# Two graph layers on one core: exps and scalings moved into later rounds, the change of layers and the end laid out anew

## The chip, the cores and the metric

The kernel runs on one core of a Trainium2 chip. The metric is the device time of one execution in microseconds; before the change the median of three runs is 2457.41 us (2450.8 to 2460.89). Engines are named as in the profile: PE multiplies matrices (PEld loads its weights), DVE is the vector engine, ACT the scalar engine, POOL is GpSimd, and SP only issues DMAs (SPq). Each engine works through its own instructions in order; across engines they wait on semaphores.

## The reference

There are 128 graphs of 128 nodes with 512 features. Layer 0 is attention with a two-step propagation, layer 1 scores every node against its graph and scales a projected value by a softmax over the nodes. All numbers are float32.

```python
# layer 0
h = relu(layernorm(x))
Xw = h @ Wv + bv;  sj = Xw @ aw[:d, 0];  si = Xw @ aw[d:, 0]
e = leaky_relu(sj[:, None, :] + si[:, :, None] + ab[0], 0.2)
alpha = A * exp(e);  transition = alpha / (sum(alpha, -1) + 1e-12)
H = 0;  Xk = h
for k in range(3):
    H = H + Xk @ Wk[k] + bk[k]
    Xk = einsum('bij,bjd->bid', transition, Xk)
x = x + relu(H)
# layer 1
h = relu(layernorm(x))
q, k = split(h @ Wqk);  v = h @ Wv1
agg = einsum('bij,bjd->bid', adj, k * mask)
w = mask / sqrt(512) * einsum('bid,bid->bi', q, agg)
x = x + softmax(w, axis=1)[:, :, None] * v
```

## The kernel before

Layer 0 goes through 64 pairs of graphs and writes to DRAM, for each pair: h of layer 1 (H2D), its transposed blocks (XD), the transposed adjacency (ATD) and x after layer 0 (X1D).

Layer 1 goes through 32 quads (two pairs, four graphs), `q` from 0 to 31. Its products h @ [M, Wv1], where M joins both score weights, are done with Strassen's scheme at two levels. The outer level has seven factors (1, 5, 2, 6, 3, 7, 4), the inner one seven products (p1, p5, p6, p2, p7, p3, p4). A quad has two rounds: the first takes factors 1 and 5 in the PSUM banks a1, b1, c1, e1 and, step by step beside it, 2 and 6 in a2, b2, c2, e2; the second takes 3 and 7, and 4. Each step is one product of both sets.

```python
def one_round(q, banks, factors, s, ends):
    ...
    def p1():
        product(a, 1, True)
        nc.scalar.copy(b, a)
    def p5():
        product(e, 5, True)
        nc.scalar.copy(s[:, 0], e)
    def p6():
        product(b, 6)
        nc.scalar.copy(c, b)
    def p2():
        product(a, 2)
        ends[0, 0](v[0])
    def p7():
        product(c, 7)
        nc.scalar.copy(s[:, 1], c)
        ends[1, 1](v[3], sv[:, 1])
    def p3():
        product(b, 3)
        ends[0, 1](v[1], sv[:, 0])
    def p4():
        product(c, 4)
        ends[1, 0](v[2])
```

The ends of set 2 are additions: DVE adds the PSUM bank into s, POOL adds that to c (`two`), or DVE adds the bank to c at once (`one`). So ACT copies between banks, and PE needs these copies for its next steps.

The left operands: `load_left(q)` loads four blocks of f by the SP queue and lets POOL form four sums; `inner_sums` lets DVE form the inner level's operands `in` from f. f has two buffers, one for even and one for odd quads.

```python
def weights(w, pw):                      # softmax factors of a quad
    nc.vector.tensor_reduce(peak, pw, AX.X, OP.max, negate=True)
    for j in range(g2):                  # four graphs
        nc.scalar.activation(ej, pw[:, j, :], AF.Exp, bias=peak[:, j:j + 1], accum_out=w[:, 2, j:j + 1])
    nc.vector.tensor_add(w[:, 3], w[:, 0], peak)
    nc.scalar.activation(w[:, 4], w[:, 3], AF.Exp)
    nc.vector.reciprocal(w[:, 5], w[:, 2])
    nc.vector.tensor_mul(w[:, 3], w[:, 4], w[:, 5])

def spread_scores(col):                  # scores to DRAM and back, to every partition: pwd, pw
    ...
def scaled(q):
    factors = weights(W.pop(q), PW.pop(q))
    for pair in range(2):
        for j in range(G):
            nc.scalar.activation(v, v, AF.Copy, scale=factors[:, at:at + 1])

def store(q):
    for pair in range(2):
        nc.gpsimd.dma_start(v, X1D[p].rearrange("g n d -> n g d"), accum_op=OP.add)   # c += x1
        nc.sync.dma_start(out[p * G:(p + 1) * G].rearrange("b n d -> n b d"), v)

for q in range(NQ):
    together(one_round(q, set1, (1, 5), ...), one_round(q, set2, (2, 6), ...))
    done["v"] = nc.gpsimd.tensor_add(outer[0], outer[3], outer[1]).ins               # "v"
    if q > 1:
        behind("v", store, q - 2)
    for i, bank in enumerate((a1, a2, e1, e2)):                                     # agg
        ordered(nc.tensor.matmul, bank, AT[q][:, pair, j], H2[q][:, pair, j], ...)
        nc.scalar.copy(agg[:, pair, j], bank)
    if q + 1 < NQ:
        load_rest(q + 1)                                                            # h2, at
        inner_sums(q + 1, early, 0, 4)
    scores(q, 0, c[:, 2])
    together(one_round(q, set1, (3, 7), ...), one_round(q, set2, (4,), ...))
    nc.gpsimd.tensor_add(outer[1], outer[3], outer[1])
    if q + 2 < NQ:
        load_left(q + 2, fpools[q % 2])
    if q + 1 < NQ:
        inner_sums(q + 1, back, 4, 3)
    scores(q, 1, c[:, 2])
    PW[q] = spread_scores(W[q])
    if q > 0:
        behind("score", scaled, q - 1)
scaled(NQ - 1)
for q in (NQ - 2, NQ - 1):
    store(q)
```

c, in which a quad's result is built, has three buffers. The order on each engine is not the order of the program text: a scheduler places the instructions by priority and by what they need, and `behind` and `ordered` hold it to an order.

Of the kernel before, what the change touches and what calls it, by code (L numbers as in the profile page):

```python
# [15 lines left out]
def kernel(  # L16
# [25 lines left out]
    nc = tc.nc  # L42
# [34 lines left out]
                                      ("a1", "b1", "c1", "e1", "a2", "b2", "c2", "e2"))  # L77
    set1, set2 = (a1, b1, c1, e1), (a2, b2, c2, e2)

    def behind(what, op, *args):  # L80

        with tc.issue_after(done[what]):
            return op(*args)

    def ordered(op, *args, **how):

# [375 lines left out]
    def y10(p, steps):  # L462

        s = front.tile([P, 2, WP * 2], FP, name="s", bufs=1)[:, :, :D]

        def end12(b, t):
            done["c12"] = behind("left" if p else "t", nc.vector.tensor_add, b, b, t).ins

        strassen(set1, LEFT.pop(p), right10, s, False, {
            (0, 0): lambda a: None,  # L470
            (1, 1): lambda e, t: behind("left" if p else "t", nc.vector.tensor_add, e, e, t),
            (0, 1): end12,
            (1, 0): lambda c: None}, steps)

# [76 lines left out]
    for p in range(NP):  # L551
        def lefts():
            if p == 0:
                behind("t", begin, 1)
                behind("left", norm0, 2)
                return
            if p + 2 < NP:
                behind("t", begin, p + 2)
            if p + 3 < NP:
                behind("left", norm0, p + 3)  # L560

        if p > 1:
            behind("x1", attention, p)
        y10(p, {1: lefts, 6: lambda: t_transposed(p)})
        if p > 0:
            behind("c12", for_layer1, p - 1)
        z = inner(p)
        if p == 0:
            y2(1)
            spread_columns(1)  # L570
            attention(1)
        outer(p, z)
        if p == 0:
            begin(2)
            norm0(3)
            setup_ctx.close()
            stage_ctx = ExitStack()
            stage = stage_ctx.enter_context(tc.tile_pool(name="stage", bufs=2, side="right"))
        if p + 2 < NP:
            y2(p + 2)  # L580
        if p + 1 < NP:
            seed_a()
            seed_e()
        norm2(p)
        if p + 4 < NP:
            load_x(p + 4)
        if p + 3 < NP:
            load_adj(p + 3)
        if p == 2:
            rightl = combine({(kh, k): rl[:, kh * HC:(kh + 1) * HC, k] for kh in range(2)  # L590
                              for k in range(2)}, [tl[:, i] for i in range(4)])
        if 3 <= p < 3 + len(FACTORS):
            prepare(FACTORS[p - 3], stage)
        if p == 3 + len(FACTORS):
            stage_ctx.close()
            prep_ctx.close()
            early = ctx.enter_context(tc.tile_pool(name="early", bufs=1, side="right"))
            RW = {}
            for o in FACTORS[:4]:
                RW[o] = early.tile([P, 7, HD], FP, name=f"rw{o}")  # L600
                nc.sync.dma_start(RW[o], RWD[o])
# [42 lines left out]
    load_left(0, early)  # L644
    inner_sums(0, early, 0, 4)
    layer0.close()
    back = ctx.enter_context(tc.tile_pool(name="back", bufs=1))
    fpools[1] = back
    for o in FACTORS[4:]:
        RW[o] = back.tile([P, 7, HD], FP, name=f"rw{o}")  # L650
        nc.sync.dma_start(RW[o], RWD[o])

    def load_rest(q):
        H2[q] = back.tile([P, 2, G, D], FP, name="h2", bufs=2)
        AT[q] = back.tile([P, 2, G, N], FP, name="at", bufs=2)
        for i in range(2):
            p = 2 * q + i
            nc.sync.dma_start(H2[q][:, i], H2D[p].rearrange("g n d -> n g d"))
            nc.sync.dma_start(AT[q][:, i], ATD[p])

    def one_round(q, banks, factors, s, ends):

# [11 lines left out]

        def p1():
            product(a, 1, True)
            nc.scalar.copy(b, a)

        def p5():
            product(e, 5, True)  # L680
            nc.scalar.copy(s[:, 0], e)

        def p6():
            product(b, 6)
            nc.scalar.copy(c, b)  # L685

        def p2():
            product(a, 2)
# [1 line left out]

        def p7():
            product(c, 7)
            nc.scalar.copy(s[:, 1], c)  # L693
            ends[1, 1](v[3], sv[:, 1])

        def p3():
# [8 lines left out]

    def plain_ends(to):

        return {(0, 0): lambda a: nc.scalar.copy(to(0, 0), a),
                (1, 1): lambda e, t: nc.vector.tensor_add(to(1, 1), e, t),
                (0, 1): lambda b, t: nc.vector.tensor_add(to(0, 1), b, t),  # L710
                (1, 0): lambda c: nc.scalar.copy(to(1, 0), c)}

    def adding_ends(to, other):

        def one(i, j):
            return lambda a: nc.vector.tensor_add(to(i, j), a, other(i, j))  # L716

        def two(i, j):
            def end(e, t):
                nc.vector.tensor_add(t, e, t)  # L720
                nc.gpsimd.tensor_add(to(i, j), t, other(i, j))  # L721
            return end

        return {(0, 0): one(0, 0), (1, 1): two(1, 1), (0, 1): two(0, 1), (1, 0): one(1, 0)}

    def together(*rounds):
        for steps in zip(*rounds):
            for step in steps:
                step()

    def weights(w, pw):

        g2 = 2 * G
        w = w[:, :6 * g2].rearrange("p (k g) -> p k g", g=g2)
        peak = small.tile([P, g2], FP, name="peak")
        nc.vector.tensor_reduce(peak, pw, AX.X, OP.max, negate=True)
        for j in range(g2):
            ej = back.tile([P, N], FP, name="ej", bufs=2)
            nc.scalar.activation(ej, pw[:, j, :], AF.Exp, bias=peak[:, j:j + 1],  # L739
                                 accum_out=w[:, 2, j:j + 1])  # L740
        nc.vector.tensor_add(w[:, 3], w[:, 0], peak)
        nc.scalar.activation(w[:, 4], w[:, 3], AF.Exp)
        nc.vector.reciprocal(w[:, 5], w[:, 2])
        nc.vector.tensor_mul(w[:, 3], w[:, 4], w[:, 5])
        return w[:, 3]

    def spread_scores(col):

# [6 lines left out]
        nc.sync.dma_start(dst.rearrange("p g n -> p (g n)"), bcast(d, 0, 2 * G * N))  # L755
        return dst

    C, W, PW = {}, {}, {}

    def scores(q, pair, y):  # L760

        for j in range(G):
            junk = back.tile([P, D], FP, name="junk", bufs=1)
            b, at = (2 * q + pair) * G + j, pair * G + j
            done["score"] = nc.vector.scalar_tensor_tensor(
                junk, agg[:, pair, j], wscale[:, b:b + 1], y[:, j].rearrange("p h d -> p (h d)"),
                op0=OP.mult, op1=OP.mult, accum_out=W[q][:, at:at + 1]).ins

    def scaled(q):

        factors = weights(W.pop(q), PW.pop(q))
        for pair in range(2):
            for j in range(G):
                v = C[q][:, pair, j].rearrange("p h d -> p (h d)")
                at = pair * G + j
                nc.scalar.activation(v, v, AF.Copy, scale=factors[:, at:at + 1])  # L776

    def store(q):

# [4 lines left out]
            nc.gpsimd.dma_start(v, X1D[p].rearrange("g n d -> n g d"), accum_op=OP.add)  # L784
            nc.sync.dma_start(out[p * G:(p + 1) * G].rearrange("b n d -> n b d"), v)

    load_rest(0)
    inner_sums(0, back, 4, 3)
    load_left(1, back)
    for q in range(NQ):  # L790

        c = C[q] = back.tile([P, 4, G, 2, HD], FP, name="c", bufs=3)
        W[q] = wcols[q % 3]
        s1 = back.tile([P, 2, D], FP, name="s1", bufs=1)
        s2 = back.tile([P, 2, D], FP, name="s2", bufs=1)
        agg = back.tile([P, 2, G, D], FP, name="agg", bufs=1)
        outer = [c[:, i].rearrange("p j h d -> p (j h d)") for i in range(4)]

        together(one_round(q, set1, (1, 5), s1, plain_ends(lambda i, j: c[:, 0:2, i, j])),
                 one_round(q, set2, (2, 6), s2, adding_ends(  # L800
                     lambda i, j: c[:, 2:4, i, j],
                     lambda i, j: c[:, 0:1, i, j].to_broadcast([P, 2, HD]))))

        done["v"] = nc.gpsimd.tensor_add(outer[0], outer[3], outer[1]).ins
        if q > 1:
            behind("v", store, q - 2)
        for i, bank in enumerate((a1, a2, e1, e2)):
            pair, j = divmod(i, 2)
            ordered(nc.tensor.matmul, bank, AT[q][:, pair, j], H2[q][:, pair, j], start=True, stop=True)
            done["agg"] = nc.scalar.copy(agg[:, pair, j], bank).ins  # L810
        if q + 1 < NQ:
            load_rest(q + 1)
            inner_sums(q + 1, early, 0, 4)
        scores(q, 0, c[:, 2])

        together(one_round(q, set1, (3, 7), s1, adding_ends(lambda i, j: c[:, 0::3, i, j],
                                                            lambda i, j: c[:, 0::3, i, j])),
                 one_round(q, set2, (4,), s2, adding_ends(lambda i, j: c[:, 2:3, i, j],
                                                          lambda i, j: c[:, 3:4, i, j])))

        nc.gpsimd.tensor_add(outer[1], outer[3], outer[1])
        if q + 2 < NQ:
            load_left(q + 2, fpools[q % 2])
        if q + 1 < NQ:
            inner_sums(q + 1, back, 4, 3)
        scores(q, 1, c[:, 2])
        PW[q] = spread_scores(W[q])
        if q > 0:
            behind("score", scaled, q - 1)
    scaled(NQ - 1)  # L830
    for q in (NQ - 2, NQ - 1):
        store(q)


# [23 lines left out]
```

## Time and profile before

One execution of the kernel before spans 2452.7 us, with a mean granted PE clock of 0.971. Busy time by engine (its share of the span counts all stages together):

| engine | busy us | share | instructions |
|---|---|---|---|
| PE | 2284.0 | 93% | 8223 |
| DVE | 1694.6 | 69% | 4191 |
| ACT | 1246.3 | 51% | 2929 |
| POOL | 865.2 | 35% | 854 |

Layer 0 lasts until about 1471 us, layer 1 from there to the end. By stretches of 300 us within layer 1 (1520 to 2420), PE is busy for 266 to 269 us, DVE for 236 to 242, ACT for 157 and POOL for 195 to 205; the granted clock is 0.95 to 0.97 there and 1.00 in layer 0 from 100 to 1440 us. In a table of windows a share is read within its own stage; a wait in brackets in the timeline gives the idle time before an instruction and what ended it.

### The profile page before, as it was taken

What the parts mean: (1) busy time and instruction counts of PE and PEld (TensorE: products, weight loads), DVE (VectorE), ACT (ScalarE), POOL (GpSimd) and SP (SyncE); (2) the same over time, 40 slices, a digit from 0 to 9 for tenths busy, and PEclk for the clock granted to TensorE, in tenths of its full rate; (3) what the DMA queues carried; (4) which work ended last, traced back from release to release, by engine and by line L of the source; (5) the groups of instructions that cost most, each with busy time, mean ns of one, the idle gap of its engine ahead of it and who ended that gap; (6) DMA issues with size and microseconds to landing.
All of it is one profiled execution on the core that took longest, in us unless ns stands there. A gap on an engine that the chain in (4) does not pass through costs nothing.

```text
span 2452.7 us, 29079 instructions
## 1 busy us (share of the span) xinstructions
PE 2284.0 (93%) x8223; PEld 1563.6 (64%) x8223; DVE 1694.6 (69%) x4191; ACT 1246.3 (51%) x2929; POOL 865.2 (35%) x854
## 2 busy tenths in 40 slices
PE   8899999999999999999999997888888889998884
PEld 4566656566666666666666665677776777777773
DVE  5676666666666666666666655878887777788784
ACT  3455545455555555555555543555555555555553
POOL 3011111211111111111111104666666666667663
PEclk8999999999999999999999998999999999899997
DMA  7566786667666666666666645466666555555665
GB/s 201 176 201 197 219 262 202 179 189 202 196 184 184 193 204 189 180 192 198 200 185 183 188 136 192 126 171 166 168 168 171 157 158 155 155 155 163 167 159 124
DMA packets 379011, 440.95 MB, mean 180 GB/s; under 512 B 35342, under 2 KB 233614, under 8 KB 378850
## 3 DMA queue, kind: packets, MB, share of 16 engines
q1 hardware_dynamic: 347344, 386.23, 51.5%
q0 software_dynamic: 31504, 52.87, 11.8%
q8 instruction: 65, 1.06, 0.2%
q14 instruction: 96, 0.79, 0.1%
q10 hardware_dynamic: 2, 0.00, 0.0%
HBM read 256.33 MB, written 182.65 MB: 179 GB/s over the span
## 4 chain that ended last, share of the span: by engine, by line
PE 73%; DVE 10%; ACT 6%; DMA 5%; issue 3%; POOL 2%; SPq 1%; ACTq 0%; POOLq 0%; DVEq 0%
PE a L88 22%; PE c L88 20%; PE b L88 19%; PE e L88 12%; DVE in L633 2%; ACT ej L739 2%; DVE s L720 2%; DMA c<-x1d 2%; DMA f<-xd 1%; POOL c L721 1%; DVE in L631 1%; ACT c L776 1%; DVE c L716 1%; DVE in L632 1%; ACT s L693 1%
## 5 line engine op out<-in xcount | busy, mean ns | idle before, releaser
L108 POOL DMA_DIRECT2D agb<-in_adj_dram x256 | 148.4, 586 | 754.9 <-DVE aT L436 712.5
L88 PE MATMUL a<-r,x 128*128 128x512 f32 (+1 forms) x1024 | 376.4, 490 | 8.7 <-DVE x L320 8.6
L721 POOL TENSOR_TENSOR c<-s,c 128x512 f32<-128x512 f32 x192 | 225.5, 1189 | 235.5 <-DVE s L720 181.2
L88 PEld LDWEIGHTS a<-r,x 128*128 128x128 f32 x1024 | 191.0, 192 | 88.9 <-issue 62.3
L88 PE MATMUL b<-rw,in 128*128 128x256 f32 x896 | 239.1, 412 | 0.0
L88 PE MATMUL a<-rw,f 128*128 128x256 f32 x896 | 214.3, 379 | 0.0
L88 PEld LDWEIGHTS b<-rw,in 128*128 128x128 f32 x896 | 187.7, 210 | 30.6
L88 PE MATMUL c<-rw,in 128*128 128x256 f32 x448 | 122.9, 406 | 85.7 <-ACT c L685 85.7
L88 PEld LDWEIGHTS a<-rw,f 128*128 128x128 f32 x896 | 170.2, 190 | 36.8 <-issue 14.6
L88 PE MATMUL b<-t,sx 128*128 128x257 f32 (+1 forms) x512 | 187.7, 489 | 4.6 <-ACT b L360 4.6
L88 PE MATMUL c<-t,x 128*128 128x257 f32 (+1 forms) x512 | 187.0, 487 | 2.5 <-ACT s L368 2.5
L88 PE MATMUL c<-t,sx 128*128 128x257 f32 (+1 forms) x512 | 188.5, 491 | 0.2 <-ACT c L364 0.2
L88 PE MATMUL e<-t,sx 128*128 128x257 f32 (+1 forms) x512 | 187.0, 488 | 0.0
L88 PE MATMUL b<-r,sx 128*128 128x257 f32 (+1 forms) x512 | 186.4, 486 | 0.0
L320 DVE STREAM_TRANSPOSE x<-hv 128x512 f32<-128x512 f32 x254 | 165.3, 688 | 23.5 <-DMA hv<-hd 13.6
L276 DVE BATCH_NORM_STATS2 st<-xg 128x6 f32<-128x512 f32 x128 | 82.3, 684 | 135.1 <-DMA xg<-in_x_dram 135.1
L88 PEld LDWEIGHTS c<-rw,in 128*128 128x128 f32 x448 | 85.8, 197 | 108.7 <-ACT c L685 97.8
L368 ACT COPY s<-c 128x257 f32<-128x257 f32 (+1 forms) x128 | 60.6, 473 | 174.5 <-PE c L88 174.2
L88 PEld LDWEIGHTS b<-t,sx 128*128 128x128 f32 x512 | 97.6, 192 | 74.4 <-issue 60.5
L88 PEld LDWEIGHTS c<-t,sx 128*128 128x128 f32 x512 | 97.5, 191 | 71.8 <-issue 61.6
L88 PEld LDWEIGHTS c<-t,x 128*128 128x128 f32 x512 | 94.6, 189 | 74.8 <-issue 60.5
L88 PEld LDWEIGHTS e<-t,sx 128*128 128x128 f32 x512 | 97.5, 190 | 68.6 <-issue 48.5
(205 smaller groups left out, 4675.9 us busy)
## 6 DMA issues: line engine op xcount, KB each, us to landing
x1d<-x SPq DMA_DIRECT2D x64, 512.0 KB, 3.8
h2d<-h SPq DMA_DIRECT2D x64, 512.0 KB, 3.7
hv<-h2d SPq DMA_DIRECT2D x256, 128.0 KB, 3.6
xd<-x SPq DMA_DIRECT2D x128, 256.0 KB, 3.2
f<-xd SPq DMA_DIRECT2D x128, 256.0 KB, 3.9
h<-h2d SPq DMA_DIRECT2D x64, 512.0 KB, 3.8
c<-x1d POOLq DMA_DIRECT2D x64, 512.0 KB, 8.7
out_dram<-c SPq DMA_DIRECT2D x64, 512.0 KB, 3.7
```

Source lines behind the costliest of these rows:

```text
L88: done["mm"] = op(*args, **how).ins
L108: nc.gpsimd.dma_start(agb[p][c * S32:(c + 1) * S32].rearrange("p g q i -> p (g q) i"), v[c])
L276: nc.vector.bn_stats(st, src[:, j, :])
L320: nc.vector.transpose(dst[:, j].rearrange("p f (n b) -> p f n b", n=Q), hv[:, j].rearrange("p n (f a) -> p f n a", f=Q))
L368: nc.scalar.copy(s[:, 1], c)
L631: nc.vector.tensor_sub(s[:, 1], s[:, 0], b[0, 0])
L632: nc.vector.tensor_sub(s[:, 2], b[0, 0], b[1, 0])
L633: nc.vector.tensor_sub(s[:, 3], b[0, 1], s[:, 1])
L693: nc.scalar.copy(s[:, 1], c)
L720: nc.vector.tensor_add(t, e, t)
L721: nc.gpsimd.tensor_add(to(i, j), t, other(i, j))
L739: nc.scalar.activation(ej, pw[:, j, :], AF.Exp, bias=peak[:, j:j + 1], accum_out=w[:, 2, j:j + 1])
```

## The change

Exps and scalings: `scaled` is taken apart. In quad q the peaks of quad q - 1 are taken after the end of the first round, its four exps follow steps 0 to 3 of the second round (each behind the last ACT copy), the factors step 4, two scalings steps 5 and 6, and the other two scalings steps 5 and 6 of the first round of quad q + 1. They are meant to stand where ACT does not hold up PE's copies.

Change of layers: h2, at and c, s of quad 0 are allocated first, and h2, at and the last three weights are loaded by ACT's queue in place of SP's.

End: the last quad is written out on its own. Its first round takes factors 1, 6 and 2, 7, its second part factors 4, 5 and 3 one by one; DVE takes the additions that POOL does elsewhere; scores are spread by PE into PSUM and not through DRAM; DVE scales and adds x1 in one instruction.

In layer 0, at pair 0, the norm of pair 2 goes before the transposes of pair 1, and the additions at the end of `y10` stand behind "rs" in place of "left".

```diff
         def end12(b, t):
-            done["c12"] = behind("left" if p else "t", nc.vector.tensor_add, b, b, t).ins
+            done["c12"] = behind("rs" if p else "t", nc.vector.tensor_add, b, b, t).ins
...
             if p == 0:
-                behind("t", begin, 1)
-                behind("left", norm0, 2)
+                behind("t", norm0, 2)
+                behind("rs", begin, 1)
...
     back = ctx.enter_context(tc.tile_pool(name="back", bufs=1))
     fpools[1] = back
+    load_rest(0, nc.scalar)
+    begin_quad(0)                       # s1, s2, c, W
     for o in FACTORS[4:]:
         RW[o] = back.tile([P, 7, HD], FP, name=f"rw{o}")
-        nc.sync.dma_start(RW[o], RWD[o])
+        nc.scalar.dma_start(RW[o], RWD[o])
...
+    def exps(w, pw, peak, at, graphs):
+        for j in graphs:
+            ej = back.tile([P, N], FP, name="ej", bufs=2)
+            behind("copy", nc.scalar.activation, ej, pw[:, j, :], AF.Exp,
+                   bias=peak[:, j:j + 1], accum_out=w[:, 2, at + j:at + j + 1])
...
+    for q in range(NQ - 1):
...
         together(one_round(q, set1, (1, 5), ...), one_round(q, set2, (2, 6), ...),
+                 {5: lambda: scale(q - 2, 1, 0), 6: lambda: scale(q - 2, 1, 1)} if q > 1 else {})
         done["v"] = nc.gpsimd.tensor_add(outer[0], outer[3], outer[1]).ins
         if q > 1:
             behind("v", store, q - 2)
+        if q > 0:
+            late = behind("end", peaks, W[q - 1], PW.pop(q - 1)) + (0,)
+        agg = aggregate(q)
...
+        work = {i: lambda i=i: exps(*late, (i,)) for i in range(4)}
+        work[4] = lambda: factors(*late)
+        work.update({i: lambda i=i: scale(q - 1, 0, i - 5) for i in (5, 6)})
         together(one_round(q, set1, (3, 7), ...), one_round(q, set2, (4,), ...),
+                 work if q > 0 else {})
...
-        if q > 0:
-            behind("score", scaled, q - 1)
-    scaled(NQ - 1)
-    for q in (NQ - 2, NQ - 1):
-        store(q)
+    q = NQ - 1
+    x1 = back.tile([P, 2, G, D], FP, name="h2", bufs=2)
...
+    together(one_round(q, set1, (1, 6), ...), one_round(q, set2, (2, 7), ..., nc.vector),
+             {2: lambda: scale(q - 2, 1, 0), 3: lambda: scale(q - 2, 1, 1), 4: last_peaks, 5: last_factors,
+              6: lambda: last_scales(0)})
+    store(q - 2)
...
+    agg = aggregate(q)
+    last_scales(1)
+    store(q - 1)
+    scores(q, 0, c[:, 2])
...
+    steps((r4, 0), (r4, 1), (r5, 0), (r4, 2), (r5, 1), (r4, 3))
+    spread_pair(0)
...
+    finish(0, 1, c[:, 1, 1], nc.sync)
```

## The prediction

> **What bounds the kernel now.** I read the table of windows first, because one busy share over the whole span mixes two layers. Its columns are: window, length, busy time of PE, PEld, DVE, ACT and POOL with instruction counts, granted clock, DMA share, GB/s.
>
> ```profile
> 400.00:1440.00 1040.00, 1037.49 (x3488) 646.00 (x3487) 680.27 (x2217) 544.23 (x1318) 168.43 (x286) 1.00 0.66 191
> ...
> 1515.90:1540.50 24.60, 24.60 (x107) 20.15 (x107) 23.93 (x32) 11.55 (x22) 18.76 (x12) 1.00 0.35 109
> ...
> 2187.70:2217.00 29.30, 26.50 (x107) 21.13 (x106) 23.75 (x36) 15.44 (x35) 20.11 (x14) 0.94 0.57 159
> ```
>
> Layer 0 has no gap on PE (1037 of 1040 us), so nothing is to be had there. In layer 1 the same PE work of one quad (four graphs) took 24.6 us in quad 1 and 29.3 us in quad 25. Quad 1 is the one that has no exps, no scalings and no store yet. So the work of PE is 24.6 us and 4.7 us per quad are lost to what came later. Note that DVE is busy for 23.9 us even in the fast quad.
>
> The waits over 1520 to 2420 (who waited for whom: us in total, times, longest) name the losers:
>
> ```profile
> POOL f L623 <- DMA f<-xd: 105.5, 28, 5.1
> ...
> PE c L88 <- ACT c L685: 85.7, 30, 4.7
> ACT ej L739 <- DVE peak L736: 74.9, 22, 5.2
> ```
>
> PE waits in one place, 30 times, 2.86 us each. The timeline of one quad shows why:
>
> ```profile
> 2195.40 0.68 DVE L736 TENSOR_REDUCE peak<-pw 128x4 f32<-128x512 f32 x1
> ...
> 2196.12 0.40 ACT L739 ACTIVATE ej<-pw,peak 128x128 f32<-128x128 f32 x1 [3.32 <-DVE peak L736]
> ...
> 2197.77 0.57 ACT L685 COPY c<-b 128x512 f32<-128x512 f32 x1
> ...
> 2198.39 1.60 PE L88 MATMUL c<-rw,in 128*128 128x256 f32 x4 [2.80 <-ACT c L685]
> 2199.11 2.56 ACT L776 ACTIVATE c<-c,wcol 128x512 f32<-128x512 f32 x4 [0.77 <-DVE wcol L744]
> 2199.79 3.15 PE L88 MATMUL b<-rw,in 128*128 128x256 f32 x8
> ```
>
> The four exps stand in ACT's order ahead of the copy c2<-b2. The first has waited 3.32 us for the peaks, which DVE takes only after the sums of the next quad. PE needs that copy, idles 2.80 us, and then runs slowly: 3.15 us for eight instructions that take 1.89 elsewhere, and 1.60 for four that take 1.03. Together 2.80 + 1.26 + 0.57 = 4.63 of the 4.7 us.
>
> The second thing to see is a ring around PE. POOL alone, for one quad:
>
> ```profile
> 2267.14 2.44 POOL L784 DMA_DIRECT2D c<-x1d  x2
> ...
> 2284.30 1.26 POOL L623 TENSOR_TENSOR f<-f 128x512 f32<-128x512 f32 x1 [3.54 <-DMA f<-xd]
> ...
> 2288.23 1.27 POOL L622 TENSOR_TENSOR f<-f 128x512 f32<-128x512 f32 x1
> 2290.64 2.50 POOL L721 TENSOR_TENSOR c<-s,c 128x512 f32<-128x512 f32 x2 [1.14 <-DVE s L720]
> 2293.21 2.68 POOL L804 TENSOR_TENSOR c<-c 128x1024 f32<-128x1024 f32 x1
> 2295.83 2.43 POOL L784 DMA_DIRECT2D c<-x1d  x2
> ```
>
> A store is issued (L784). The SP queue holds the output writes until those adding DMAs have landed, and behind them the loads of f. POOL waits for f, makes its four sums, adds the ends of the first round, makes v, and only then issues the next store. From store to store it is 28.69 us here, with only 1.14 us of slack in it.
>
> The tail is the last thing read: its last two adding DMAs in POOL's timeline, held back by the scalings on ACT:
>
> ```profile
> 2436.73 1.20 POOL L784 DMA_DIRECT2D c<-x1d  x1 [3.22 <-ACT c L776]
> 2438.18 1.20 POOL L784 DMA_DIRECT2D c<-x1d  x1 [0.24 <-issue]
> ```
>
> PE's last matmuls end near 2419.6; scores, a round trip through DRAM, exps, scalings, adding DMAs and output writes follow, 33 us to the end at 2452.7.
>
> **What the Trainium skill says.** (1) "TensorE: Matmul & The Clock Gate", part 1 on the HAM clock gate: an idle window of about 3.4 us drops the clock to half and sustained work restores it. The trace agrees in kind: the granted clock is 0.94 in a quad with the gap and 1.00 in quad 1; the slow stretch appears after an idle time of only 2.80 us. (2) "ScalarE: Activation LUTs", on what ACT_TABLE_LOAD costs: about 280 ns + 0.833 ns per element with a pointer operand, an estimate of 387 ns for an exp of 128 and 707 for a scaling of 512; the trace has 390 and 710. (3) "SBUF — State Buffer", two separate sides: GpSimd and a VectorE instruction with two SBUF inputs share a port pair under an exclusive lock. The trace agrees: the score product L765 takes 0.74 us alone and 2.94 at 2409.21, beside POOL's 2.35 us addition. (4) "DMA: Bandwidth & Descriptors", SWDGE vs HWDGE: an adding DMA can only be issued from GpSimd, so stores stay in POOL's order; no run here tries another way.
>
> **The change, part by part.**
> Exps and scalings. Nothing is removed from ACT: 4 x (0.39 + 0.19) + 0.19 + 4 x 0.71 = 5.4 us per quad stay. The exps now follow the copies of the second round's first steps, one per step, two scalings end that round and two the next quad's first round. The peaks now come between the quad's two rounds. ACT's busy time of 15.4 us leaves room, and a step of PE lasts 1.3 us or more, longer than one exp with its read (0.58). I take the 4.63 us of PE's wait as removed.
>
> What takes its place is the ring. By its terms: store to f ready 17.2 us (the mean of 28 quads in POOL's timeline, 15.8 to 18.8); four sums 5.2; two ends 2.5; v 2.65. Sum 27.5 us. The new order of the SP queue puts one more h2 load between output writes and f, but takes it out of the time in which the adding DMAs run; I count that as even. Then DVE: in the new order its sums in<-f (which need POOL's) stand ahead of the last end c<-c2, which v needs. With the port lock they take 1 to 2.8 us each here, so v can start up to 0.8 us late. I take +0.4: 27.9 us per quad against 29.3 now, with PE idle for some 3 us still, now behind POOL. Over the 28 intervals from the store in quad 2 to that in quad 30: 28 x 1.4 = 39 us.
>
> Change of layers. Before, PE has two gaps, 9.2 us (1481.7 to 1490.9, behind s<-c, freed by the last xd write) and 6.1 us plus slow matmuls (to 1500.7, behind h2 and at, which were queued after three weight loads). Now h2 and at go first, on ACT's queue, but they still wait for all of layer 0, and ACT spends some 3.4 us on seven issues (that is what the same seven took SP from 1488.75: 1.29 + 0.66 + 0.47 + 0.50 + 0.47) before it copies s. I expect 5 us less. The first store then comes earlier: in quad 2 it was at +24.1 us of the quad's start (1540.5 to 1564.6), pushed out by a stall of 4.67; now +17 (six steps of 1.73 to the end of p3, 1.4 for two additions on DVE, 2.5 + 2.65 on POOL). That is 7 us more. Together 12.
>
> The end. From the store of quad 30 (2382.8) to the end is 69.9 us. New: quad 31 begins some 3 us after that store. Its DVE order has the peaks of quad 30 in the middle of the first round, and their scores go through DRAM behind an output write on the SP queue, which itself waits for an adding DMA issued only at about +7.5. So peaks at about +21, the copies that free a1 and e1 at +25 to +27, PE idle for about 6 us; then 21 single products of 0.43 us with copies between them, about 13 us; then the last scaled addition and an output write, 1.2 + 0.8 + 3.5. Sum about 49: 21 us less. In the last quad DVE adds x1 together with the scaling, so no adding DMA stands at the end.
>
> Layer 0. Only the order at pair 0 and of the end additions moves; PE has no gap after 100 us. The 8.6 us gap at 73 to 82 ends with transposes of DVE that still stand behind the sums tl. Zero.
>
> Sum: 12 + 39 + 21 = 72 us; 2457.4 - 72 = 2385 us.
>
> **The rivals.** (a) PE free: the ring gives way and a quad takes 24.6 to 25.5 us. Then 28 x 4 = 112 us in place of 39, about 2310. For it speaks quad 1; against it that this quad has no store, and that the terms of the ring are all measured. (b) DVE is the bound: 23.9 us busy in a quad plus its waits for POOL's sums and for the output write to free c. The order makes DVE wait 3 us or more at in<-f; a quad would be 28.5 to 29, and only the end and the entry gain: about 2415 to 2425. For it speak the 1 to 2.8 us that the port lock costs. (c) DMA: between store and f the engines are over 90% busy; if all transfers slow each other, 17.2 rises to 18.5 and the quad stays above 28.7, again about 2410. (d) The end costs as much as before, through the wait for peaks: plus 15.
>
> **Range and chances.** The quad is the large term: 0.8 us either way is 22 us; the ends add 12. So 2345 to 2415. Faster by over 2% means below 2408: 0.79. Within 2%: 0.18. Slower by over 2% would need a new wait of 4 us per quad beyond all those above: 0.03.
>
> **What would show it.** PE's wait for c<-b behind exps gone, and ACT's waits for peaks gone; store to store near 27.9 us, with POOL's f<-xd wait still there each quad and next to no idle time before the ends' addition; PE idle of about 3 us in the second round behind an ACT copy that waits for POOL; the clock still below 1; PE's end to the span's end below 10 us. Wrong would be: quads of 25 us (ring not closed), quads of 29 with DVE waiting for POOL (rival b), or a last quad over 55 us.

## The result, and the profile after

The changed kernel takes 2428.4 us (median of four runs, 2424.7 to 2429.9) against 2458.3 for the kernel before on the same chip: a ratio of 0.988, 95% interval 0.986 to 0.991. Predicted were 2385 us and a range of 2345 to 2415. The change made the kernel faster by about 1.2%, not by 3%, and the time lies outside the range. In the profiled executions (2452.7 and 2428.1 us) the difference splits into four stretches; the landmarks are PE's first matmul of layer 1, its first matmul of quad 1, and the store that POOL issues in quad 30 (it holds quad 28's result):

| stretch | before, us | after, us | difference | predicted |
|---|---|---|---|---|
| start to layer 1's first matmul | 1471.2 | 1484.8 | +13.7 | 0 |
| quad 0, to the first matmul of quad 1 | 44.8 | 45.9 | +1.2 | -5 |
| quad 1, to the store in quad 30 | 866.9 | 848.2 | -18.7 | -46 |
| store in quad 30 to the end | 69.9 | 49.1 | -20.8 | -21 |
| all | 2452.7 | 2428.1 | -24.6 | -72 |

The table of windows, for layer 0, quad 1 and one period of the steady stretch, here from the end of one wait of PE to about the end of the next (window, length, busy time of PE, PEld, DVE, ACT and POOL, granted clock, DMA share, GB/s):

```profile
400.00:1440.00 1040.00, 1038.58 (x3481) 642.97 (x3480) 672.97 (x2209) 555.43 (x1315) 169.03 (x286) 1.00 0.64 191
1530.76:1555.34 24.58, 24.58 (x107) 20.14 (x106) 24.48 (x34) 13.24 (x31) 18.44 (x12) 1.00 0.33 108
2145.40:2174.25 28.85, 25.23 (x106) 19.58 (x106) 23.55 (x36) 15.07 (x35) 20.04 (x15) 1.00 0.60 165
```

Quad 1 again runs at PE's pace, 24.6 us. A quad in the steady stretch is still over 28 us: PE is busy for 25.2 of 28.85. Over quads 3 to 30 the mean is 28.67 us, where it was 29.28.

The waits over 1520 to 2380 (who waited for whom: us in total, times, longest):

```profile
POOL f L623 <- DMA f<-xd: 151.4, 23, 8.2
DVE in L630 <- POOL f L621: 128.4, 28, 6.1
ACT ej L83 <- DVE peak L757: 94.5, 29, 4.6
...
PE c L88 <- ACT c L673: 68.1, 28, 3.7
```

POOL's wait for f has grown from 105.5 to 151.4 us: a ring is still closed there. But ACT's wait for peaks has grown too (74.9 before), and PE still waits behind it, 28 times. The timeline of one quad, with lines of POOL, DVE, ACT and PE put in order of time:

```profile
2164.32 1.26 POOL L623 TENSOR_TENSOR f<-f 128x512 f32<-128x512 f32 x1 [7.01 <-DMA f<-xd]
...
2168.20 0.69 DVE L630 TENSOR_TENSOR in<-f 128x512 f32<-128x512 f32 x1 [4.90 <-POOL f L621]
...
2171.09 0.67 DVE L757 TENSOR_REDUCE peak<-pw 128x4 f32<-128x512 f32 x1
...
2171.80 0.40 ACT L83 ACTIVATE ej<-pw,peak 128x128 f32<-128x128 f32 x1 [3.90 <-DVE peak L757]
...
2173.61 0.85 ACT L673 COPY c<-b 128x512 f32<-128x512 f32 x2
...
2174.25 2.77 PE L88 MATMUL c<-rw,in 128*128 128x256 f32 x6 [2.92 <-ACT c L673]
```

Read it upwards. PE wants c<-b, which stands on ACT behind the first exps; the first exp waits for the peaks; the peaks stand on DVE behind in<-f; in<-f waits for POOL's sums; POOL waits for f. So the old wait is there again, with another cause at its root: the transfer of f. POOL by itself, from one store to the next:

```profile
2146.54 2.44 POOL L805 DMA_DIRECT2D c<-x1d  x2
...
2168.24 1.78 POOL L622 TENSOR_TENSOR f<-f 128x512 f32<-128x512 f32 x1
2169.98 2.93 POOL L737 TENSOR_TENSOR c<-s,c 128x512 f32<-128x512 f32 x2
2172.99 2.68 POOL L832 TENSOR_TENSOR c<-c 128x1024 f32<-128x1024 f32 x1
2175.61 2.44 POOL L805 DMA_DIRECT2D c<-x1d  x2
```

From f's landing to the next store no line has an idle time in brackets: the ring has no slack left, and it is 29.07 us long here. In all 28 intervals POOL idles for 0.08 us between f's landing and the next store; in the kernel before the mean was 1.49 us. The fourth sum (L622) takes 1.78 us where it took 1.27; DVE's in<-f begins beside it at 2168.20.

Between the store at 2146.54 and f's landing stands the queue of SyncE, which holds the output writes until the adding DMAs have landed (from 1560 to 2380 us it waits for them 56 times, 455 us in all) and has the loads of f behind them:

```profile
2153.40 3.24 SPq L806 DMA_DIRECT2D out_dram<-c  x2
...
2158.18 1.83 SPq L618 DMA_DIRECT2D f<-xd  x4
```

The end went as predicted, and step by step. Counted from the store in quad 30, quad 31 begins at +2.6 us (+3 predicted), the peaks of quad 30 come at +21.9 (+21), the copies that free a1 and e1 at +24.7 to +27.9 (+25 to +27), and PE's last matmul ends 8.4 us before the span's end (below 10). It is DVE that now adds x1 while it scales (h<-c,wcol,h, the output's last addition), so no adding DMA stands behind PE's last matmuls. The queue of SyncE and DVE at the end:

```profile
2421.45 3.98 SPq L920 DMA_DIRECT2D out_dram<-h  x3
...
2423.67 1.40 DVE L918 SCALAR_TENSOR_TENSOR h<-c,wcol,h 128x512 f32<-128x512 f32 x2
```

Two losses stand where the prediction had a gain of 5 us and a zero. At the change of layers ACT's own queue, then ACT itself, and PE behind it:

```profile
1502.13 0.41 ACTq L663 DMA_DIRECT2D h<-h2d  x1
...
1506.73 0.33 ACTq L664 DMA_DIRECT2D at<-atd  x1
1507.10 4.61 ACTq L670 DMA_DIRECT2D rw<-rwd  x3
1511.75 1.07 ACT L673 COPY s<-e 128x512 f32<-128x512 f32 x2 [19.71 <-DMA h<-h2d]
...
1513.86 3.78 PE L88 MATMUL c<-rw,f 128*128 128x256 f32 x8 [18.50 <-ACT s L673]
```

From the first issue to the copy 9.6 us pass; PE stands for 18.5 us in one piece, where it stood for 9.2 and 6.1 before. And in layer 0, where nothing was expected, the waits of PE up to 400 us have a line that the kernel before does not have: the additions of layer 0's products (e<-e,s), three times, 7.5 us. One of them, on DVE and PE:

```profile
305.83 0.16 DVE L283 TENSOR_TENSOR r<-r 128x2 f32<-128x2 f32 x1 [5.19 <-ACT r L282]
...
306.62 0.16 DVE L288 SCALAR_TENSOR_TENSOR rs<-mv,rs 128x2 f32<-128x2 f32 x1
306.69 0.69 DVE L83 TENSOR_TENSOR e<-e,s 128x512 f32<-128x512 f32 x1
...
307.44 1.22 PE L88 MATMUL e<-y,tt 128*128 128x256 f32 x2 [2.49 <-DVE e L83]
```

The addition that PE waits for stands on DVE behind the statistics rs of a later pair, and these wait for ACT.

### The profile page after: what moved, and what is told of

The parts are those of the page before. It is cut to its first block, busy times and chain, and to the rows that moved or that the text cites. A ratio compares the mean times of both kernels' runs of the same rounds, so it can differ in the third digit from the quotient of the medians.

```text
span 2428.1 us, 29205 instructions
## 1 busy us (share of the span) xinstructions
PE 2285.2 (94%) x8227; PEld 1553.5 (64%) x8227; DVE 1710.4 (70%) x4210; ACT 1259.0 (52%) x2932; POOL 865.2 (36%) x844
## 4 chain that ended last, share of the span: by engine, by line
PE 65%; DMA 10%; POOL 10%; DVE 6%; issue 4%; ACT 2%; SPq 2%; POOLq 0%; ACTq 0%; DVEq 0%
PE c L88 18%; PE a L88 18%; PE b L88 18%; PE e L88 10%; DMA f<-xd 5%; DMA c<-x1d 4%; POOL c L737 3%; POOL f L621 1%; POOL f L623 1%; POOL f L620 1%; DVE junk L795 1%; POOL c L832 1%; POOL c L851 1%; SPq L618 1%; DVE c L731 1%
## 5 line engine op out<-in xcount | busy, mean ns | idle before, releaser
L737 POOL TENSOR_TENSOR c<-s,c 128x512 f32<-128x512 f32 (+1 forms) x186 | 220.9, 1201 | 61.1 <-DVE s L736 54.6
L88 PE MATMUL b<-rw,in 128*128 128x256 f32 x896 | 227.3, 395 | 11.1 <-ACT b L673 11.1
L88 PEld LDWEIGHTS b<-rw,in 128*128 128x128 f32 x896 | 177.2, 199 | 44.2 <-ACT b L673 18.1
L88 PE MATMUL c<-t,x 128*128 128x257 f32 (+1 forms) x512 | 192.2, 498 | 2.0 <-ACT s L368 1.6
L795 DVE SCALAR_TENSOR_TENSOR junk<-agg,wscale,c 128x512 f32<-128x512 f32 x128 | 160.1, 1251 | 3.6 <-POOL c L737 2.3
L630 DVE TENSOR_TENSOR in<-f 128x512 f32<-128x512 f32 x64 | 53.5, 836 | 140.1 <-POOL f L621 137.5
```

The source lines that it names most:

```text
L88: done["mm"] = op(*args, **how).ins
L630: nc.vector.tensor_add(s[:, 0], b[1, 0], b[1, 1])
L737: engine.tensor_add(to(i, j), t, other(i, j))
L795: nc.vector.scalar_tensor_tensor(junk, agg[:, pair, j], wscale[:, b:b + 1], y[:, j].rearrange("p h d -> p (h d)"), op0=OP.mult, op1=OP.mul ...
```

## The experiments

All but three start from the changed kernel. Each was timed on one chip beside the kernel before, and the ratios are to it. The first four look at one suspected loss each. In the edits, "..." stands for lines left out.

**Layer 0's additions, in another place.** The change tied them behind rs; here they are tied behind the sums of left factors, which come earlier.

```diff
-            done["c12"] = behind("rs" if p else "t", nc.vector.tensor_add, b, b, t).ins
+            done["c12"] = behind("left" if p else "t", nc.vector.tensor_add, b, b, t).ins
...
-            (1, 1): lambda e, t: behind("rs" if p else "t", nc.vector.tensor_add, e, e, t),
+            (1, 1): lambda e, t: behind("left" if p else "t", nc.vector.tensor_add, e, e, t),
```

> The changed kernel, with the additions at the end of y10 put back behind left in place of rs (pairs after the first). Theory: in layer 0 these additions now stand behind the norm of a pair whose x comes late when stages and weights are loaded at pairs 7 to 13, and PE waited 2.5 us three times for them, with a slow clock after it. Then layer 1 begins about 8 to 10 us earlier than in the changed kernel (1484.8), pairs 11 to 13 take about 22.4 us each as before in place of 26.4, and the whole takes about 2419. Rival: the three long pairs come from the loads themselves or from where they fall in this run; then the pairs stay long and the time stays at 2428.

Measured: 2416.1 us, ratio 0.983 (0.980 to 0.987). From its first product a<-r,x of pair 10 to that of pair 14 PE needs 90.1 us, as in the kernel before, where it needed 100.4 in the changed kernel, and its wait for e<-e,s is gone. So 10.3 of the 13.7 us of layer 0 are this order. Another 2.8 us lay ahead of pair 1 (its first product at 67.6 us against 64.8), and that start moves by itself: it was between 58.8 and 67.6 us in the eight runs that begin as the changed kernel does. About 0.5 us are left over.

**The output writes behind the loads of f.** The store is split: POOL's adding DMA stays where it was, the output write goes onto the queue of SyncE only behind the loads of f. Nothing is computed otherwise. (`store` now takes two flags, for its adding DMA and for its output write; `"f"` is the last load of f.)

```diff
...
-            behind("v", store, q - 2)
+            behind("v", store, q - 2, True, False)
...
             load_left(q + 2, fpools[q % 2])
+        if q > 1:
+            behind("f", store, q - 2, False, True)
```

> The changed kernel, with the output writes of a store queued on SP behind the loads of f in place of ahead of them; nothing else. Ring theory (store, output writes, f, POOL's sums, ends, v, next store holds a quad at 28.67 us): f comes as soon as PE has freed its buffer, POOL's wait for f goes, and a quad takes 25 to 26 us; the whole about 2340 to 2355. DVE theory (DVE's 24 us and its waits hold the quad): the quad stays at 28 us or more, the whole at 2415 to 2428.

Measured: 2318.6 us, ratio 0.945 (0.941 to 0.948), 110 us less than the changed kernel. The mean quad falls from 28.67 to 24.87 us. In the profiled executions the difference is 114 us: 28 quads make 106 of it, and 8.6 are an earlier start of layer 1, which this edit does not touch. One window of its profile, then POOL and the queue of SyncE in its timeline:

```profile
1600.00:2300.00 700.00, 689.64 (x2940) 557.29 (x2938) 662.86 (x981) 432.72 (x985) 566.23 (x383) 0.99 0.68 189
```

```profile
2013.80 2.44 POOL L806 DMA_DIRECT2D c<-x1d  x2
2019.04 4.30 POOL L737 TENSOR_TENSOR c<-s,c 128x512 f32<-128x512 f32 x4 [2.80 <-DVE s L736]
2019.82 1.86 SPq L618 DMA_DIRECT2D f<-xd  x4
2021.80 1.58 SPq L808 DMA_DIRECT2D out_dram<-c  x2
2023.30 2.65 POOL L853 TENSOR_TENSOR c<-c 128x1024 f32<-128x1024 f32 x1
2025.92 1.58 POOL L623 TENSOR_TENSOR f<-f 128x512 f32<-128x512 f32 x1
```

PE is busy for 690 of 700 us, DVE for 663. In POOL's line of the first sum (L623) the bracket with the wait for f is gone: f has landed before POOL asks, and POOL now waits for DVE instead, at no cost. The theory that DVE bounds the quad falls with this. It was better than the ring theory had it, for a reason that the upward reading above gives: with f early, in<-f does not hold the peaks either, and from 1600 to 2300 us ACT's wait for them drops from 83.5 to 12.5 us.

**The ring made longer.** One of POOL's four sums is computed twice from quad 4 on (to the same place, so only time is added).

```diff
         nc.gpsimd.tensor_sub(at[7], at[1], fv[:, L21])
+        if q > 3:
+            nc.gpsimd.tensor_sub(at[7], at[1], fv[:, L21])
```

> The changed kernel with one of POOL's four sums of f done twice in each quad from 4 on: 1.27 us more on POOL, where POOL works from f's landing to the store without a pause. Ring theory: every quad grows by 1.27 to 1.8 us, 28 quads by 36 to 50 us: about 2464 to 2478. If DVE or PE holds the quad and POOL's chain has slack, under 15 us.

Measured: 2459.6 us, 31 more than the changed kernel, ratio 1.001 (1.000 to 1.002). The closed ring was expected to cost at least 36 us; in the profiled execution layer 1 began 4.4 us earlier than in the changed kernel's, which hides a part. The interval between stores grows from 28.67 to 29.93 us, by 1.26, which is the length of that one sum (L625):

```profile
2068.47 1.26 POOL L623 TENSOR_TENSOR f<-f 128x512 f32<-128x512 f32 x1 [7.48 <-DMA f<-xd]
2069.82 1.26 POOL L625 TENSOR_TENSOR f<-f 128x512 f32<-128x512 f32 x1
```

What is put into POOL's part of the ring comes out in the quad; had there been slack, it would not have.

**The first loads of layer 1 off ACT.** The loads of h2 and at for quad 0 and of three weights go to the queue of SyncE.

```diff
-    load_rest(0, nc.scalar)
+    load_rest(0, nc.sync)
...
-        nc.scalar.dma_start(RW[o], RWD[o])
+        nc.sync.dma_start(RW[o], RWD[o])
```

> The changed kernel with h2, at and the last three weights of the change of layers issued by SP again (h2 and at first), so that ACT issues none. Theory: PE's gap of 18.5 us before the last step of the first round is ACT being held by its seven issues from 1502.1 to 1511.7; without them ACT copies s at about 1502.5, the gap falls to about 9, and layer 1 is about 8 us earlier from then on: about 2420. Rival: the loads themselves set the pace (h2, at, then 2.75 MB of weights), the gap only moves behind the aggregation or to the second round: 2426 to 2428.

Measured: 2415.3 us, ratio 0.984 (0.981 to 0.987). PE's timeline at the change of layers:

```profile
1497.05 3.78 PE L88 MATMUL c<-rw,f 128*128 128x256 f32 x8 [8.92 <-ACT s L673]
...
1508.21 1.19 PE L88 MATMUL a<-rw,f 128*128 128x256 f32 x2 [1.97 <-DMA rw<-rwd]
```

The gap is 8.92 us in place of 18.50: the 9.6 us that ACT had spent at its queue are off PE's path. About four of them come back in quad 0's second round, which now waits for weights and runs behind. Quad 0 is 40.6 us long in place of 45.9: 5.4 us less. The remaining difference in the time is mostly layer 0's start, by which layer 1 began 7.2 us earlier in this run than in the changed kernel's; it must not be credited to the edit.

**All three edits.**

> The three edits together: the output writes behind the loads of f, layer 0's additions behind the two sums of left factors, and the first loads of h and at and the last three weights on the queue of SyncE. If the three losses are separate stretches of the time (layer 0 12 us, the change of layers 10 us, the ring 110 us), they add up: the ring edit alone gave 2318.5, less 12 and less 10 makes 2296 (2288 to 2304). If they hide one another, for instance because an earlier start only moves the wait to the ring, the time stays above 2308.

Measured: 2304.3 us, ratio 0.938 (0.936 to 0.940): faster than both kernels, and 6% below the one before. Against the run with the output writes alone the profiled span is 13.1 us shorter: layer 1 starts 8.4 us earlier and quad 0 is 5.8 us shorter. They add up; the time is above the expectation by what the two edits had been overrated, 4 us each.

**The kernel before, with the output writes behind f.** This tells whether the exps had to be moved at all. The edit is that of the second experiment, applied to the kernel before.

> The kernel before with the ring edit alone (output writes behind the loads of f), its exps and scalings still in one block. If PE's gap of 4.6 us behind the block was the second wall at nearly the same height, PE needs 24.6 + 4.6 = 29.2 us a quad and nothing is gained: 2445 to 2460. If the block only stood in the shadow of the ring, so that the gap shrinks once f comes early, the quad falls to 25 to 27 us and the time to 2345 to 2400; then the placing of the exps would have been unneeded.

Measured: 2513.2 us, ratio 1.022 (1.020 to 1.025). Slower, and neither branch expected that. DVE, ACT and PE in its timeline:

```profile
2048.03 1.75 DVE L765 SCALAR_TENSOR_TENSOR junk<-agg,wscale,c 128x512 f32<-128x512 f32 x1
...
2049.83 1.62 DVE L765 SCALAR_TENSOR_TENSOR junk<-agg,wscale,c 128x512 f32<-128x512 f32 x1
...
2052.10 0.40 ACT L739 ACTIVATE ej<-pw,peak 128x128 f32<-128x128 f32 x1 [5.21 <-DVE peak L736]
...
2054.37 2.07 PE L88 MATMUL c<-rw,in 128*128 128x256 f32 x4 [4.68 <-ACT c L685]
```

POOL's sums of f now come early, and so beside the two score products of DVE, which take 1.75 and 1.62 us in place of 0.74 and 0.75. The peaks stand behind these products, so the exps start 1.9 us later and PE's gap is 4.68 us in place of 2.80. The quad goes from 29.28 to 31.24 us, by 2.0. In the mean of a quad PE idles for 1.35 us more and loses 0.68 us more to slow matmuls behind it. So an earlier f made DVE's path to the peaks longer, and that path was the bound. This is read from the trace; no run takes the slower products away by themselves.

**The kernel before, with the exps asked for earlier.** The whole block of peaks, exps and scalings is asked for ahead of the second scores; the scheduler then spreads the exps between ACT's copies by itself (wcol stands for the last small product on DVE that the scalings need). Once with the output writes behind f as well, once without.

```diff
...
-        scores(q, 1, c[:, 2])
+        if q > 0:
+            behind("score", scaled, q - 1)
+            behind("wcol", scores, q, 1, c[:, 2])
+        else:
+            scores(q, 1, c[:, 2])
         PW[q] = spread_scores(W[q])
-        if q > 0:
-            behind("score", scaled, q - 1)
```

> The kernel before with two edits alone: the output writes behind the loads of f, and the peaks, exps and scalings of the last quad asked for ahead of the second scores in place of behind them (ACT's order then has the exps between the copies of the second round, and DVE's has the peaks ahead of that round's ends). Its layer 0, its change of layers and its end stay as they were. Two walls of nearly equal height: with both gone a quad takes 24.5 to 25.5 us in place of 29.3, which is 28 x 4.3 = 120 us less: 2330 to 2350. If the loss of the run with the ring edit alone came from something else (transfers, the memory of the output writes), this one keeps quads of 28 us or more and a time above 2430.

> The kernel before with the exps moved alone, by the same edit of the order, and the ring closed as it was. PE's gap behind the exps goes, the ring holds the quad at its own length: 27.5 + 0.8 for the sums beside DVE = 28.3 to 28.9 us, which is 2430 to 2450. If PE's gap alone had been the bound, the quad would be 25 us and the time below 2350.

Measured: 2446.0 us with both (0.996, 0.995 to 0.997) and 2498.3 us with the exps alone (1.018, 1.015 to 1.020). Both expectations missed, by 100 and 50 us, and the theory behind them, that the exps only had to be spread, falls. ACT and PE of the first of the two, then of the second:

```profile
2037.01 0.40 ACT L739 ACTIVATE ej<-pw,peak 128x128 f32<-128x128 f32 x1 [4.23 <-DVE peak L736]
...
2039.55 2.33 PE L88 MATMUL c<-rw,in 128*128 128x256 f32 x6 [3.35 <-ACT c L685]
```

```profile
2025.42 0.40 ACT L739 ACTIVATE ej<-pw,peak 128x128 f32<-128x128 f32 x1 [5.37 <-DVE peak L736]
...
2026.44 2.93 PE L88 MATMUL b<-rw,in 128*128 128x256 f32 x6 [4.43 <-ACT b L677]
```

The exps are spread, and yet the first one holds ACT for 4 to 5 us, since on DVE the peaks still stand behind in<-f and two scores. One exp that waits holds all copies behind it just as well as four.

**A block again, but with early peaks.** From the run with all three edits; the four exps stand in one block behind the first copies of the second round. The peaks stay behind the last end of the first round, where the change has them.

```diff
-        work = {i: lambda i=i: exps(*late, (i,)) for i in range(4)}
+        work = {0: lambda: exps(*late, range(4))}
```

> The run with all three edits, and in it the four exps in one block behind the first step's copies of the second round in place of one behind each of four steps; the peaks stay where the change put them, ahead of the block. If the peaks' early place is what counts, and 'one per step' is a matter of fit: the block takes 2.3 us, the copies c<-b end at about 24.5 us of the quad's time line in place of 23.3, PE wants them at 24.04, so it waits 0.5 to 1.0 us a quad: 14 to 28 us more, 2318 to 2332. If a block as such costs what the kernel before paid (4.6 us a quad), the time goes up by some 120 us to 2420.

Measured: 2308.2 us, ratio 0.938 (0.934 to 0.942), against 2304.3 and the same 0.938 (0.936 to 0.940): no difference to be seen, and the 14 to 28 us that even the milder branch expected did not appear. The block is there in ACT's timeline, with no wait ahead of it:

```profile
2022.88 0.85 ACT L673 COPY b<-a 128x512 f32<-128x512 f32 x2 [0.28 <-PE a L88]
2023.63 0.42 ACT L83 ACTIVATE ej<-pw,peak 128x128 f32<-128x128 f32 x1
...
2024.80 0.40 ACT L83 ACTIVATE ej<-pw,peak 128x128 f32<-128x128 f32 x1
...
2025.19 0.85 ACT L673 COPY s<-e 128x512 f32<-128x512 f32 x2
```

**One per step, but with late peaks.** The counterpart: the run with all three edits, where only DVE's reduction for the peaks is moved, behind the first two scores. ACT's order does not change (score stands for the second of these two products).

```diff
-        if q > 0:
-            late = behind("end", peaks, W[q - 1], PW.pop(q - 1)) + (0,)
         agg = aggregate(q)
...
         scores(q, 0, c[:, 2])
+        if q > 0:
+            late = behind("score", peaks, W[q - 1], PW.pop(q - 1)) + (0,)
```

> The run with all three edits, with one thing moved: DVE takes the peaks behind the first two scores in place of behind the last end of the first round. ACT's order is the same line for line, one exp per step. If the peaks' place on DVE is the second wall, the first exp waits some 4 us for them ahead of the copies s<-e and c<-b, PE gets a gap of about 3.4 us and slow matmuls behind it as in the run with two edits of the kernel before (29.0 us a quad), and the time goes up by 28 x 4.3 = 120 us to 2410 to 2440. If spreading the exps over the steps is what takes the wait off PE, the peaks may come late: 2300 to 2325.

Measured: 2409.3 us, ratio 0.979 (0.974 to 0.984), 105 us more for one instruction of 0.68 us moved. The quad is 28.35 us; 28 quads make 100 us of the difference. ACT and PE in its timeline:

```profile
2015.63 0.40 ACT L83 ACTIVATE ej<-pw,peak 128x128 f32<-128x128 f32 x1 [4.65 <-DVE peak L757]
...
2017.80 2.93 PE L88 MATMUL c<-rw,in 128*128 128x256 f32 x6 [3.38 <-ACT c L673]
```

The table puts the quads together. There are two walls of nearly the same height, the ring and the late peaks:

| mean quad, us | output write ahead of f | output write behind f |
|---|---|---|
| peaks behind in<-f and scores, exps in a block | 29.28 (before) | 31.24 |
| the same, exps spread by the scheduler | 30.84 | 29.03 |
| peaks behind scores, exps one per step | not run | 28.35 |
| peaks behind the last end, one per step | 28.67 (the change) | 24.76 to 24.87 |
| peaks behind the last end, in a block | not run | 24.93 |

In the two last rows the traces have one or two of DVE's in<-f ahead of that last end. This is why the changed kernel's peaks wait for f, and why an early f frees them.

## Why the prediction was wrong, by its steps

The step that failed most is the ring: its terms added up to 27.9 us and measured 28.72, so the quads gave 14 us in place of 39. With layer 0 (13.7 us), the change of layers (6.2) and the first store (2.5) this makes the 47 us by which the profiled difference fell short of 72.

- "Layer 0 ... Zero": wrong, +13.7 us. PE had no gap there, and the step took this to mean that an order of DVE could not cost anything. The new tie behind rs made one: 10.3 us, taken back by the first experiment. The rest is the start, which varies by itself (2.8), and 0.5 us that stay open.
- "I expect 5 us less" at the change of layers: wrong, +1.2 us. It took seven issues on ACT as 3.4 us, from their length on another queue. On ACT the copy stood behind them for 9.6 us; that part came off PE's path in the fourth experiment. The Trainium skill's "DMA: Bandwidth & Descriptors", in "Issuing engines are not separate DMA queues", says that issuing from several engines saves only the sequencer's time, usually small beside the DMA. Here it cost PE 9.6 us, since ACT had copies to run behind its issues.
- The ring, 27.9 us: the mechanism was right (the third experiment), some terms were too small. Measured, as means of the 28 intervals: store to f 17.41 (17.2 predicted), the four sums 5.69 (5.2), ends and v 5.62 (5.15, plus 0.4 for DVE). Together 28.72. The mis-sized term is mostly the sums, 0.5 of the 0.8 us. The 0.4 us for the port lock were put on DVE's side, but POOL's last sum is longer as well, 1.77 us in place of 1.27 in the mean. In the traces the new order lets in<-f begin in the middle of the sums, and only the sum beside it is longer; no run moves in<-f away to test it. From the store in quad 2 to that in quad 30 the interval fell from 29.22 to 28.72 us: 14 us in place of 39.
- The first store at +17 us of its quad: it came at +19.6, so 4.5 us in place of 7.
- "ACT's waits for peaks gone": wrong. They are 94.5 us. The prediction saw that in<-f would wait for POOL in the new order, and did not see that the peaks, and through them ACT and PE, stand behind in<-f. In the changed kernel this costs nothing by itself, since the ring is as long anyway; the tenth experiment shows what it costs otherwise.
- "PE idle of about 3 us in the second round": nearly right, 2.92 us in the quad shown and 2.43 in the mean of 28 waits, but by way of the peaks.
- "I take the 4.63 us of PE's wait as removed": wrong, since the idle time came back by way of the peaks. The 4.63 us were also those of one quad with a slow stretch; over 27 quads of the kernel before the mean is 3.11 us idle and 1.33 us of slow matmuls, 4.44 together.
- The end, 49 us: right, 49.1, and rival (d) falls with it.
- Rival (a), a free PE, was held off by the ring, as written; with the ring opened its 24.6 to 25.5 us came about. Rival (b), DVE, falls: DVE does its work in 24.8 us a quad. Rival (c), slower transfers, falls for the most part: 17.41 us against 17.2.

## What to carry to other kernels

When a wait sits in front of a block of work, look at what the first instruction of the block waits for before the block is broken up: here, with early peaks, the spreading was worth nothing (24.76 and 24.93 us a quad), and the place of one reduction on another engine some 100 us. Where loads and writes share a queue, put the loads that the next round needs ahead of writes that wait for something; that was some 106 us by order alone. In the kernel before, with its late peaks in a block, the same order cost 2 us a quad. And an engine without gaps is no proof that an order on its suppliers is free: it only says that the present order is.

## What the runs showed of the hardware

- Matmuls behind an idle time of PE can run at half pace for a while (0.427 us from one start to the next in place of 0.216), mostly for about 3 us. The same idle time does not always bring it: of 29 idle times of 2.79 to 2.81 us in the kernel before, 18 were followed by five or more such matmuls, at once or up to 1.8 us later, and 11 by none. Behind 3.99 to 4.62 us, in the run with the exps alone, all 29 were. A much longer idle time was no worse: eight matmuls took 3.78 us behind 18.50 us as behind 8.92, and 1.89 otherwise.
- GpSimd and VectorE slow each other in both directions on 128x512 additions and products in fp32: in the run with the output writes behind f POOL's four sums take 1.53 to 1.61 us in the mean (1.27 for the first three in the changed kernel), and DVE's score products 1.75 beside such sums (kernel before with early f) and 2.83 beside POOL's 128x1024 addition (changed kernel), in place of 0.74.
- Three weight loads held ACT's queue for 4.61 us; on the queue of SyncE the same three took 1.38 us in the run with all three edits. Why they took longer on ACT stays open.
